# A GRU behind three residual layers on one core: the loads of the prologue in another order and on other queues, and one unit instead of two beside the z projection

## The chip, the core and the metric

The kernel runs on one core of one Trainium2 chip. A core has a TensorE (PE in the profile; PEld is its weight load), a VectorE (DVE), a ScalarE (ACT), a GpSimd (POOL) and a SyncE (SP), each of which works through its own instructions in the order in which the program lists them, and 16 DMA engines that are shared by all queues. The metric is the device time of one execution in microseconds; lower is better.

## The reference

The input x is 8 sequences of 512 tokens with 256 features. Four residual layers follow each other; three of them work on each token alone (given the conditioning vector of its sequence), the last is a recurrence over time.

```python
x = x + L0(x, cond)   # shared expert silu(x w1) * (x w3) w2, plus 8 experts gelu(x rw1) rw2,
                      # of which a router picks 2 for each token; all divided by 3
x = x + L1(x, cond)   # a Haar transform whose coefficients are all scaled by one gate(cond): x * (1 + gate)
x = x + L2(x, cond)   # x + gelu(x (down + low rank of cond)) (up + low rank of cond)
def step(H, xs):      # L3, for each of the 512 tokens
    xz, xr, xh = xs
    Z = sigmoid(xz + H @ Whz.T + bhz)
    R = sigmoid(xr + H @ Whr.T + bhr)
    H_tilda = tanh(xh + R * H @ Whh.T + bhh)
    H_new = Z * H + (1 - Z) * H_tilda
    return H_new, H_new @ Whq.T + bhq
x = x + L3(x)
```

## The kernel before

**Tiling.** Features lie on the partitions (two halves of 128), all 8 sequences are worked on together. Time is cut into 16 windows of 32 tokens (`WS`), so one window is 256 columns. L0 to L2 of one window are 72 *units* of TensorE work (`UNITS`): a unit is one call of `quads` (line 443 in its helper), four matmuls that fill the four column groups of the array, 8 matmul records with 256 columns in the trace. Layer 3 needs the windows in order, four tokens at a time.

**Two schedules.** The program is written out flat at build time. In the *prologue* (before line 1110) every instruction is a `Job` with its engine, its dependencies and the time that it is thought to take. `jobs.run(until)` plays a clock forward: each engine takes the first job of its list whose inputs are due by that clock, and the order so found is the order in the program. A load is thought to take `mb / RATE` us on its queue and to land `LAG` = 2.5 us later. The chip keeps this order, whatever the real times are: an engine whose next instruction waits does not look at the one behind it.

The prologue ends, in the plan, when window 0's last L0 matmul, the low-rank weights of L2 (`got_low_in`), the weights `wx` and `wh` and all 16 small loads `got_small` are done. Then the recurrence's own tiles are set up (lines 1110 to 1128 on DVE), window 0 is finished, three further PE jobs (`AHEAD`) are let through, the first two groups of four tokens are projected, and step 0 begins.

In the *loop*, each of the 512 steps lists its own chain, and fills the holes with jobs of later windows:

- matmuls of gate R (16 records, `grh<-wh,s_h`), sigmoid (line 1300), two transposes (1314), product with h (1331); matmuls of gate Z (16 records, `gz<-wh,s_h`) beside it;
- *first hole of PE*: one unit if `behind(s)`, and in every second step (`ahead` even) the part of the projection that feeds R and the candidate (8 records with 128 columns, `grh<-wx,xt`);
- matmuls of the candidate (16 records, `grh<-wh,s_rh`), tanh, transposes, and the scan (1390) that gives the new h;
- *second hole of PE*: in the other steps (`ahead` odd) z's part of the projection (8 records with 64 columns, `gz<-wx,xt`), and then two units if `behind(s)`, else one.

`behind(s)` is true while window 1 is unfinished, or while more units are left than a straight line that reaches zero near step 462 allows.

**Loads before.** All loads of the prologue are issued by SP (line 316), one after the other: `cond`, `rout`, `rbias` (small); x of windows 0 to 3 in two halves of 512 KB (`load_x`, rows of 512 B); `vec`, `b2` (small); `sw13` (two of 512 KB); `wsq_a` (1280 KB); `sw2`; `rw1`; `rw2`; eight pieces of `w2` (1024 KB each, line 316, into five buffers, so the sixth waits for a buffer that the first `generate` at line 1042 frees); `wx`, `wh`; 16 small loads (`h0`, `brows`, the recurrence's start and its biases); x of the other 12 windows.

**The route.** The router's logits of windows 0 to 3 (line 793) need all four windows of x; some 25 small DVE operations (lines 838 to 863) make the combination weights `s`, PE turns them (870), POOL writes them to DRAM (884) and fetches them back, broadcast (`bc`, 479). Every product of a routed expert on POOL (587) needs `bc`, and every unit `acc<-g,rw_sb` on PE needs such a product.

Of the kernel before, what the change touches and what calls it, by code (L numbers as in the profile page):

```python
# [9 lines left out]
F32 = mybir.dt.float32  # L10
# [6 lines left out]
P = 128  # L17
B, T, C = 8, 512, 256
KC = C // P
E = 8  # L20
HS = 512
HC = HS // P
R = 8
BR = B * R
WS = 32
# [7 lines left out]
FQ = C // NQ  # L33
# [18 lines left out]
EARLY = 4  # L52
# [4 lines left out]
LAST = 462  # L57
# [2 lines left out]
PE_ALONE, PE_WOVEN = 0.43, 0.65  # L60
LEAD = 20
AHEAD = 3
RATE = 0.35
LAG = 2.5


# [133 lines left out]
def cond_resid_kernel(  # L200
# [29 lines left out]
    nc = tc.nc  # L230
# [21 lines left out]
    const = ctx.enter_context(tc.tile_pool(name="const", bufs=1))  # L252
# [56 lines left out]

    jobs = Jobs()  # L310

    def load(out, in_, mb, lazies=(), deps=()):

        return jobs.add(
            "SP",
            lambda: nc.sync.dma_start(  # L316
                out=out.get() if isinstance(out, Lazy) else out, in_=in_
            ),
            deps,
            lazies,  # L320
            max(0.45, mb / RATE),
            lag=LAG,
        )

    def rows_of(m):
        return m.rearrange("(k p) o -> p k o", p=P)
# [3 lines left out]
    b2 = set1.tile([P, C], F32, name="b2")  # L330
# [3 lines left out]
    cond = const.tile([P, KC, B], F32, name="cond")  # L334
    rout = const.tile([P, 2, KC, E], F32, name="rout")
    vec = const.tile([P, 6, KC], F32, name="vec")
    rbias = const.tile([P, E], F32, name="rbias")
    got_cond = load(cond, condT, 0)
    got_rout = load(rout, router, 0)
    got_rbias = load(rbias, router_bias.broadcast_to([P, E]), 0)  # L340


    xw, xg, got_x = [], [], []
    xs, outs_ = [
        a.rearrange("(k p) (b t) -> p k b t", p=P, t=T) for a in (xT, outT)
    ]

    def load_x(n, mb):
        t0 = len(xw) * WS
        t = const.tile([P, KC, B, n * WS], F32, name=f"x{len(xg)}")  # L350
        xg.append((t0, t))
        for k in range(KC):
            got = load(t[:, k], xs[:, k, :, t0 : t0 + n * WS], mb)
        xw.extend(t[:, :, :, ts(i, WS)] for i in range(n))
        got_x.extend([got] * n)

    load_x(EARLY, 1.2)
    got_vec = load(vec, vecs, 0)
    got_b2 = load(b2[: 4 * R], bias2.rearrange("q (r d) -> (q r) d", d=C), 0)
    sw13_sb = const.tile([P, 2, KC, HS], F32, name="sw13_sb")  # L360
    got_sw13 = [load(sw13_sb[:, g], rows_of(sw13[g]), 0.5) for g in range(2)]
    wsq_a = const.tile([P, KC, 5, C], F32, name="wsq_a")
    got_sq_a = load(wsq_a.rearrange("p k n o -> p k (n o)"), rows_of(sq_a), 1.28)
    sw2_sb = const.tile([P, HC, C], F32, name="sw2_sb")
    got_sw2 = load(sw2_sb, rows_of(sw2), 0.5)
    rw1_sb = const.tile([P, KC, E, P], F32, name="rw1_sb")
    got_rw1 = load(rw1_sb.rearrange("p k e h -> p k (e h)"), rows_of(rw1), 1.0)
    rw2_sb = const.tile([P, E, C], F32, name="rw2_sb")
    got_rw2 = load(rw2_sb.rearrange("p e d -> p (e d)"), rw2, 1.0)

# [21 lines left out]
    h0 = const.tile([P, KC, B], F32, name="h0")  # L392
    brows = [const.tile([P, 3, FQ], F32, name=f"brow{n}") for n in range(2)]
    got_small = []
    for j in range(NQ):
        for i in range(KC):
            at_f = 64 * (j % 2) + 32 * i
            got_small.append(
                load(h0[ts(j, 32), i, :], condT[at_f : at_f + 32, j // 2, :], 0)
            )  # L400

        for n in range(2):
            row = bias_rows[:, 3 * n * C : 3 * (n + 1) * C].rearrange(
                "o (g f) -> o g f", g=3
            )[:, :, ts(j, FQ)]
            got_small.append(load(brows[n][ts(j, 32)], row.broadcast_to([32, 3, FQ]), 0))
    load_x(NW - EARLY, 1.8)


# [318 lines left out]
    def pe(fn, deps, lazies=(), takes=0.3):  # L728
        return jobs.add("PE", fn, deps, lazies, takes)

    def dve(fn, deps, lazies=(), takes=0.25):
        return jobs.add("DVE", fn, deps, lazies, takes)

    def act(fn, deps, lazies=(), takes=0.3):
        return jobs.add("ACT", fn, deps, lazies, takes)

    def flat(z):
        t = z.get()
        return t if len(t.shape) == 2 else t.rearrange("p a b -> p (a b)")
# [3 lines left out]
    j = dve(  # L743
        lambda: tt(
            prod,
            rout[:, 1].rearrange("p k (o e) -> p k o e", o=1).broadcast_to([P, KC, B, E]),
            cond.rearrange("p k (b o) -> p k b o", o=1).broadcast_to([P, KC, B, E]),
            ALU.mult,
        ),
        [got_cond, got_rout],  # L750
    )
# [12 lines left out]
    j = pe(time_bias, [j], [tb_ps])  # L764
# [141 lines left out]
    def mean_over_features(src, dep):  # L906
        ps = Lazy(r_c)

        def products():
            for k in range(KC):  # L910
                nc.tensor.matmul(
                    ps.get()[:, :B], inv_c, src[:, k, :], start=(k == 0), stop=(k == KC - 1)
                )

        return ps, pe(products, [dep], [ps])

    mu, j = mean_over_features(cond, got_cond)
    diff = set1.tile([P, KC, B], F32, name="diff")

    def center():  # L920
# [3 lines left out]
    j = dve(center, [j], [mu], 0.4)  # L924
    dsq = set1.tile([P, KC, B], F32, name="dsq")
    j = dve(lambda: tt(dsq, diff, diff, ALU.mult), [j])
    var_ps, j = mean_over_features(dsq, j)
    var = set1.tile([P, B], F32, name="var")
    j = dve(
        lambda: nc.vector.tensor_scalar(var, var_ps.get()[:, :B], EPS_LN, None, ALU.add),  # L930
        [j],
        [var_ps],
    )

    sd0 = set1.tile([P, B], F32, name="sd0")
    j = act(lambda: nc.scalar.activation(sd0, var, AF.Sqrt), [j], (), 1.6)
# [24 lines left out]
    def dense_cond(w, src, bias, name, dep):  # L961

        ps = Lazy(r_c)
        pre = set1.tile([P, KC, B], F32, name=f"{name}_pre")

        def out(m):
            return ps.get()[:, m * B : (m + 1) * B]

        def products():
            for m in range(KC):  # L970
                for k in range(KC):
                    nc.tensor.matmul(
                        out(m),
                        wsq_a[:, k, w, ts(m, P)],
                        src[:, k, :],
                        start=(k == 0),
                        stop=(k == KC - 1),
                    )

        def add_bias():  # L980
            for m in range(KC):
                nc.vector.tensor_scalar(
                    pre[:, m, :], out(m), vec[:, bias, m : m + 1], None, ALU.add
                )

        j = pe(products, [dep, got_sq_a], [ps], 0.6)
        return pre, dve(add_bias, [j, got_vec], [ps], 0.4)
# [6 lines left out]
    hid_pre, j = dense_cond(A_L2W1, lnc, V_BIAS1, "hid", got_lnc)  # L994
    hid_e, j = gated(hid_pre, AF.Erf, RSQRT2, "hid_e", j)
# [10 lines left out]
    g1_pre, j = dense_cond(A_L1W1, cond, V_B1, "g1", got_cond)  # L1006
    g1, j = gated(g1_pre, AF.Sigmoid, 1.0, "g1", j)
    j = dve(lambda: tt(g1, g1, g1_pre, ALU.mult), [j])
    gate_pre, j = dense_cond(A_L1W2, g1, V_B2, "gate", j)
    gate, j = gated(gate_pre, AF.Sigmoid, 1.0, "gate", j)  # L1010
# [8 lines left out]
    for n, of in enumerate(LOW):  # L1019
# [14 lines left out]
        j = pe(biased_rows, [got_b2], [gp], 0.45)  # L1034
        for k in range(KC):
            got = [pieces[q, k] for q in of]

            def generate(k=k, of=of, gp=gp):
# [12 lines left out]
            j = pe(  # L1051
                generate,
                [j, got_hid, *(g[1] for g in got)],
                [gp, *(g[0] for g in got)],
                1.75,
            )
        j = got_low_out[n] = dve(
            lambda n=n, gp=gp: nc.vector.tensor_copy(low_out[:, n], flat(gp)[:, :C]),
            [j],
            [gp],  # L1060
            0.45,
        )
# [8 lines left out]
        j = pe(turn, [j], [lt], 0.6)  # L1071
# [33 lines left out]
    with (  # L1105
# [14 lines left out]
        for u in range(GS):  # L1120
            s = gw.tile([P, KC, GS, B, 2], F32, name=f"s_h{u}")
            nc.vector.memset(s, 0.0)
            s_h.append(s)
            s = gw.tile([P, KC, GS, B], F32, name=f"s_rh{u}")
            nc.vector.memset(s, 0.0)
            s_rh.append(s)
            s = gw.tile([P, KC, B, 2], F32, name=f"d0_{u}")
# [133 lines left out]
        readers = {}  # L1261
        all_left = jobs.left("PE")

        def behind(s):
            return (
                any(j.done is None for j in ends[1])
                or jobs.left("PE") > all_left * (LAST - s) / (LAST + LEAD)
            )

        def late(s):  # L1270
# [12 lines left out]
        for c in range(NTC):  # L1283
            hist = hists[c]
            gates = upcoming
            for t in range(TC):
                s = c * TC + t
                n, u = t // GS, t % GS
                v = (u + 1) % GS
                rh, z = gates  # L1290
                now = base + s * STEP
# [28 lines left out]
                h = s_h[u][:, :, u, :, 1]  # L1320
# [3 lines left out]
                r, act_r = gate(rh[:, n, 0], AF.Sigmoid, "r", KC)  # L1324
# [27 lines left out]
                ahead = s + 5  # L1352
# [23 lines left out]
                cand, act_c = gate(rh[:, n, 1], AF.Tanh, "c", KC)  # L1376
                if part is not None:
                    part()
                jobs.fill("PE", now + 1.44, 2 if behind(s) else 1)
                if bias_parts and t >= 7:  # L1380
                    biased.append(bias_parts.pop(0)())
                    if not bias_parts:
# [27 lines left out]
                if c == NTC - 1 and t in (TC // 2 - 1, TC - TAIL - 1):  # L1410
                    a = 0 if t < TC // 2 else TC // 2
# [71 lines left out]
```

## Time and profile before

| what | us |
|---|---|
| median of 3 runs (1344.78, 1344.92, 1350.88) | 1344.92 |
| the profiled execution, its own time | 1344.15 |
| its span, first to last instruction | 1342.3 |
| first matmul of step 0 starts at | 71.90 |
| first matmul of step 511 starts at | 1334.07 |

Busy time of the span: PE 1176.8 us (88%), DVE 913.2 (68%), ACT 504.5 (38%), POOL 137.3 (10%). A share near 90% does not by itself say that PE sets the time: in the loop, PE can be busy with units that would fit elsewhere just as well. What sets the time is read stage by stage, from what ends last. The stages add up: 71.90 us of prologue, 1262.17 us for 511 steps (2.470 each), 8.23 us for the last step and the last stores, 1.85 us outside the span.

Granted PE clock and DMA, by stretch (the columns are the stretch, its length, busy us and count for each engine, then the granted clock, the mean share of the DMA engines and GB/s):

```profile
4.00:8.00 4.00, 2.86 (x20) 1.86 (x12) 1.09 (x7) 0.00 (x0) 0.00 (x0) 1.00 1.07 282
8.00:12.00 4.00, 3.43 (x145) 2.55 (x149) 2.73 (x14) 1.75 (x3) 0.00 (x0) 0.60 1.06 387
12.00:22.40 10.40, 7.87 (x121) 4.51 (x113) 6.00 (x32) 1.36 (x4) 0.00 (x0) 0.99 1.03 405
22.40:29.40 7.00, 6.50 (x60) 3.38 (x52) 2.16 (x9) 0.49 (x2) 1.82 (x3) 0.51 1.01 419
29.40:72.00 42.60, 39.93 (x728) 23.30 (x724) 12.06 (x43) 6.15 (x17) 8.11 (x12) 1.00 0.79 270
```

PE works at about half its clock from 22.4 to 29.4 us, and the DMA engines are full from 4 to about 30 us.

### The profile page before, as it was taken

The page shows a single profiled execution, that of the slowest core. Times are in us where ns is not written, and L with a number is a line of the kernel's source. Part 1 is how long each engine was busy: PE and PEld are TensorE (multiplying, and loading weights), DVE is VectorE, ACT ScalarE, POOL GpSimd, SP SyncE. Part 2 cuts the span into 40 slices and gives each one's busy share as a digit, 9 for nine tenths or more (in the row PEclk, how much of TensorE's full clock was granted, in tenths as well). Part 3 has the DMA queues.
Part 4 walks back from the last instruction along what each step waited for, and adds up shares of the span by engine and source line. Part 5 has one row for each costly group of instructions (what it writes and reads, how often), then busy time and mean ns, then how long its engine had stood idle before and what let it go on. Part 6 is the DMA issues. An engine that isn't in the chain of part 4 may idle for free.

```text
span 1342.3 us, 89396 instructions
## 1 busy us (share of the span) xinstructions
PE 1176.8 (88%) x39468; PEld 706.5 (53%) x39468; DVE 913.2 (68%) x6253; ACT 504.5 (38%) x3402; POOL 137.3 (10%) x203
## 2 busy tenths in 40 slices
PE   8999998989898989988898888889888888888885
PEld 4555555555555555554454545545555454545554
DVE  4266777776776767676676767667676766767675
ACT  1133334333343434334333433433343343433332
POOL 0211110101011110101011010101101010110000
PEclk8999999999999999999999999999999999999997
DMA  9731001100101010100101001010100100000111
GB/s 348 234 107 36 5 5 37 52 5 5 36 18 38 5 36 4 28 28 5 35 5 36 4 8 32 4 35 5 36 4 8 32 5 4 4 4 4 35 36 18
DMA packets 47093, 46.49 MB, mean 35 GB/s; under 512 B 24064, under 2 KB 44000, under 8 KB 45296
## 3 DMA queue, kind: packets, MB, share of 16 engines
q1 hardware_dynamic: 45344, 38.59, 9.3%
q8 instruction: 308, 5.05, 1.5%
q0 software_dynamic: 320, 2.13, 0.4%
q14 instruction: 81, 0.66, 0.2%
q10 hardware_dynamic: 1040, 0.07, 0.0%
HBM read 36.45 MB, written 4.33 MB: 30 GB/s over the span
## 4 chain that ended last, share of the span: by engine, by line
PE 68%; DVE 17%; ACT 8%; issue 5%; DMA 1%; SPq 1%; DVEq 0%; ACTq 0%
PE grh L1134 33%; PE hp L443 14%; PE acc L443 7%; DVE rT L1314 6%; PE gz L1134 5%; DVE d L1314 5%; PE low L443 5%; ACT r L1300 4%; PE misc L443 3%; ACT c L1300 3%; DVE s_rh L1331 2%; DVE s_h L1390 2%; SPq L316 1%; DMA wh<-in_sq_b_dram 1%; DMA x<-in_xT_dram 0%
## 5 line engine op out<-in xcount | busy, mean ns | idle before, releaser
L1300 ACT ACTIVATE r<-grh 128x32 f32<-128x32 f32 x1024 | 146.2, 195 | 443.2 <-PE grh L1134 443.2
L1314 DVE STREAM_TRANSPOSE rT<-r 128x32 f32<-128x32 f32 x1024 | 155.9, 190 | 227.6 <-ACT r L1300 224.3
L1134 PE MATMUL grh<-wh,s_h 128*32 128x64 f32 x8192 | 223.3, 226 | 78.6 <-DVE s_h L1390 76.3
L1134 PEld LDWEIGHTS grh<-wh,s_h 128*32 128x32 f32 x8192 | 143.5, 110 | 268.7 <-DVE s_h L1390 265.8
L1134 PE MATMUL grh<-wh,s_rh 128*32 128x64 f32 x8192 | 223.1, 226 | 57.6 <-DVE s_rh L1331 33.3
L1300 ACT ACTIVATE c<-grh 128x32 f32<-128x32 f32 x1024 | 146.2, 195 | 315.2 <-PE grh L1134 313.0
L1134 PEld LDWEIGHTS grh<-wh,s_rh 128*32 128x32 f32 x8192 | 141.1, 108 | 208.0 <-DVE s_rh L1331 202.1
L1314 DVE STREAM_TRANSPOSE d<-c 128x32 f32<-128x32 f32 x1024 | 156.6, 192 | 123.4 <-ACT c L1300 117.0
L1134 PE MATMUL gz<-wh,s_h 128*32 128x64 f32 x8192 | 211.3, 220 | 2.9 <-issue 2.9
L1134 PEld LDWEIGHTS gz<-wh,s_h 128*32 128x32 f32 x8192 | 154.8, 111 | 3.6 <-issue 3.6
L443 PE MATMUL hp<-x,sw_sb 128*32 128x256 f32 x2016 | 149.7, 385 | 3.6 <-issue 2.0
L443 PE MATMUL hp<-x,rw_sb 128*32 128x256 f32 x2016 | 151.0, 380 | 1.8 <-ACT sig L571 0.6
L587 POOL TENSOR_TENSOR g<-gl,bc 128x256 f32<-128x256 f32 x128 | 93.7, 733 | 546.7 <-DVE s_h L1390 379.5
L443 PE MATMUL acc<-g,rw_sb 128*32 128x256 f32 x2048 | 148.9, 379 | 0.0
L1390 DVE TENSOR_TENSOR_SCAN s_h<-d,d 128x16 f32<-128x16 f32 x1024 | 145.2, 184 | 0.0
L1331 DVE TENSOR_TENSOR s_rh<-rT,s_h 128x8 f32<-128x8 f32 x1024 | 133.5, 168 | 0.0
L1314 DVE STREAM_TRANSPOSE zT<-z 128x64 f32<-128x64 f32 x512 | 121.7, 238 | 2.9 <-ACT z L1300 2.9
L1300 ACT ACTIVATE z<-gz 128x64 f32<-128x64 f32 x512 | 121.0, 236 | 3.5 <-PE gz L1134 3.3
L1134 PE MATMUL grh<-wx,xt 128*32 128x128 f32 x2048 | 107.1, 274 | 3.1 <-ACT r L1300 3.1
L1404 ACT COPY hist<-s_h 128x16 f32<-128x16 f32 x512 | 106.1, 207 | 0.5 <-DVE s_h L1390 0.5
L1343 DVE TENSOR_TENSOR d<-zT,s_h 128x16 f32<-128x16 f32 x512 | 90.5, 177 | 17.6
L1344 DVE TENSOR_SCALAR d<-zT 128x16 f32<-128x16 f32 x512 | 86.6, 169 | 0.0
(150 smaller groups left out, 1185.5 us busy)
## 6 DMA issues: line engine op xcount, KB each, us to landing
bc<-comb_d SPq DMA_DIRECT2D x56, 256.0 KB, 4.4
w<-in_w_dram SPq DMA_DIRECT2D x8, 1024.0 KB, 17.2
out_dram<-x SPq DMA_DIRECT2D x14, 256.0 KB, 3.3
x<-in_xT_dram SPq DMA_DIRECT2D x2, 1536.0 KB, 9.7
rw_sb<-in_rw_dram SPq DMA_DIRECT2D x2, 1024.0 KB, 13.3
bc<-comb_d POOLq DMA_DIRECT2D x2, 1024.0 KB, 10.7
sw_sb<-in_sw_dram SPq DMA_DIRECT2D x3, 512.0 KB, 5.6
wsq_a<-in_sq_a_dram SPq DMA_DIRECT2D x1, 1280.0 KB, 9.5
```

The lines of the kernel that those rows point to most:

```text
L316: lambda: nc.sync.dma_start(out=out.get() if isinstance(out, Lazy) else out, in_=in_),
L443: nc.tensor.matmul(out[ts(j, 32)], lhs[:, ts(j, 32)], rhs, start=start, stop=False, skip_group_check=True,)
L587: lambda gl=gl, g=g, e=e: nc.gpsimd.tensor_tensor(g.get().rearrange("p (h t) -> p h t", t=P), gl.get().rearrange("p (h t) -> p h t", t=P), ...
L1134: nc.tensor.matmul(out[ts(j, 32)], lhs, rhs[:, ..., ts(j, FQ)], start=start, stop=False, skip_group_check=True,)
L1300: nc.scalar.activation(x, y, func)
L1314: ins = nc.vector.transpose(dst.rearrange("p i u b -> p i (u b)"), src.rearrange("p (i r) -> p i r", r=32),)
L1331: prod = tt(s_rh[u][:, k, u, :], rT[:, k, u, :], h[:, k], ALU.mult)
L1343: tt(d1[:, :, u, :, 1], zT[:, :, u, :], h, ALU.mult)
L1344: nc.vector.tensor_scalar(d0[:, :, :, 1], zT[:, :, u, :], -1.0, 1.0, ALU.mult, ALU.add)
L1390: new = nc.vector.tensor_tensor_scan(s_h[v][:, k, v].rearrange("p b w -> p (b w)"), d0[:, k].rearrange("p b w -> p (b w)"), d1[:, k, u].re ...
L1404: nc.scalar.copy(hist[:, :, t, :], s_h[v][:, :, v, :, 1])
```

## The change

Loads: the small ones of the start (`cond`, `rout`, `rbias`, `vec`, `b2`) go to ACT's queue, the 16 small ones of the end (`h0`, `brows`) to POOL's. On SP, window 0's x comes alone and first (two halves, rows of 128 B), then `sw13`, then x of windows 1 to 3 (rows of 384 B), then `rw1`, `sw2`, `wsq_a`, `rw2` (before: `wsq_a`, `sw2`, `rw1`, `rw2`). `RATE`, the planner's bandwidth, goes from 0.35 to 0.40. Loop: in the second hole, a step with z's part takes two units only if it is behind by more than 8 units (or window 1 is unfinished), else one.

```diff
-RATE = 0.35
+RATE = 0.40
...
-    def load(out, in_, mb, lazies=(), deps=()):
+    def load(out, in_, mb, lazies=(), eng="SP"):
+        issue = {"SP": nc.sync, "ACT": nc.scalar, "POOL": nc.gpsimd}[eng].dma_start
         return jobs.add(
-            "SP",
-            lambda: nc.sync.dma_start(
-                out=out.get() if isinstance(out, Lazy) else out, in_=in_
-            ),
-            deps,
+            eng,
+            lambda: issue(out=out.get() if isinstance(out, Lazy) else out, in_=in_),
+            (),
             lazies,
-            max(0.45, mb / RATE),
+            max(1.0 if eng == "POOL" else 0.45, mb / RATE),
             lag=LAG,
         )
...
-    got_cond = load(cond, condT, 0)
-    got_rout = load(rout, router, 0)
-    got_rbias = load(rbias, router_bias.broadcast_to([P, E]), 0)
+    got_cond = load(cond, condT, 0, eng="ACT")
+    got_rout = load(rout, router, 0, eng="ACT")
+    got_rbias = load(rbias, router_bias.broadcast_to([P, E]), 0, eng="ACT")
...
-    load_x(EARLY, 1.2)
-    got_vec = load(vec, vecs, 0)
-    got_b2 = load(b2[: 4 * R], bias2.rearrange("q (r d) -> (q r) d", d=C), 0)
+    x0 = const.tile([P, KC, B, EARLY * WS], F32, name="x0")
+    xg.append((0, x0))
+    xw.extend(x0[:, :, :, ts(i, WS)] for i in range(EARLY))
+    load_x(0, 0.25, (0, 1))
     sw13_sb = const.tile([P, 2, KC, HS], F32, name="sw13_sb")
     got_sw13 = [load(sw13_sb[:, g], rows_of(sw13[g]), 0.5) for g in range(2)]
+    load_x(0, 0.4, (1, EARLY))
+    got_vec = load(vec, vecs, 0, eng="ACT")
+    got_b2 = load(b2[: 4 * R], bias2.rearrange("q (r d) -> (q r) d", d=C), 0, eng="ACT")
+    rw1_sb = const.tile([P, KC, E, P], F32, name="rw1_sb")
+    got_rw1 = load(rw1_sb.rearrange("p k e h -> p k (e h)"), rows_of(rw1), 1.0)
+    sw2_sb = const.tile([P, HC, C], F32, name="sw2_sb")
+    got_sw2 = load(sw2_sb, rows_of(sw2), 0.5)
     wsq_a = const.tile([P, KC, 5, C], F32, name="wsq_a")
     got_sq_a = load(wsq_a.rearrange("p k n o -> p k (n o)"), rows_of(sq_a), 1.28)
-    sw2_sb = const.tile([P, HC, C], F32, name="sw2_sb")
-    got_sw2 = load(sw2_sb, rows_of(sw2), 0.5)
-    rw1_sb = const.tile([P, KC, E, P], F32, name="rw1_sb")
-    got_rw1 = load(rw1_sb.rearrange("p k e h -> p k (e h)"), rows_of(rw1), 1.0)
...
-                load(h0[ts(j, 32), i, :], condT[at_f : at_f + 32, j // 2, :], 0)
+                load(h0[ts(j, 32), i, :], condT[at_f : at_f + 32, j // 2, :], 0, eng="POOL")
...
-            got_small.append(load(brows[n][ts(j, 32)], row.broadcast_to([32, 3, FQ]), 0))
+            got_small.append(
+                load(brows[n][ts(j, 32)], row.broadcast_to([32, 3, FQ]), 0, eng="POOL")
+            )
...
-        def behind(s):
+        def behind(s, by=0):
             return (
                 any(j.done is None for j in ends[1])
-                or jobs.left("PE") > all_left * (LAST - s) / (LAST + LEAD)
+                or jobs.left("PE") > all_left * (LAST - s) / (LAST + LEAD) + by
             )
...
-                jobs.fill("PE", now + 1.44, 2 if behind(s) else 1)
+                two = behind(s, 8) or ahead % 2 == 0 and behind(s)
+                jobs.fill("PE", now + 1.44, 2 if two else 1)
```

## The prediction

> **What bounds the kernel now.** I cut the profiled execution at step 0 and step 511 (the starts of the first `grh<-wh,s_h` matmul of each, 71.90 and 1334.07 us) and ask of each stage what ends last.
>
> *The loop* comes first, since it holds 94% of the span. The chain of waits of the page gives most of it to PE:
>
> ```profile
> PE 68%; DVE 17%; ACT 8%; issue 5%; DMA 1%; SPq 1%; DVEq 0%; ACTq 0%
> ```
>
> That is a trap, and the timeline of PE alone, taken in a quiet stretch, shows it (columns: start, us, what, records; in brackets the idle time before and who ended it):
>
> ```profile
> 641.17 0.43 PE L1134 MATMUL grh<-wh,s_h 128*32 128x64 f32 x16 [0.36 <-DVE s_h L1390]
> ...
> 642.37 0.43 PE L1134 MATMUL grh<-wh,s_rh 128*32 128x64 f32 x16
> 642.62 0.29 PE L1134 MATMUL gz<-wx,xt 128*32 128x64 f32 x8
> 642.73 1.05 PE L443 MATMUL acc<-g,rw_sb 128*32 128x256 f32 x16
> 643.59 0.43 PE L1134 MATMUL grh<-wh,s_h 128*32 128x64 f32 x16
> ...
> 646.01 0.43 PE L1134 MATMUL grh<-wh,s_h 128*32 128x64 f32 x16 [0.36 <-DVE s_h L1390]
> ...
> 648.42 0.43 PE L1134 MATMUL grh<-wh,s_h 128*32 128x64 f32 x16 [0.24 <-DVE s_h L1390]
> ```
>
> Steps start at 641.17, 643.59, 646.01, 648.42: 2.42 us each, though the first has z's part and two units in its second hole, the third z's part and one. Over all steps the median is 2.418 and three quarters lie under 2.45. The recurrence's own chain sets the period; PE fills it. In the first of these steps the hole is exactly full: 0.25 + 0.11 + 2 x 0.43 = 1.22 us from the candidate's matmuls to the next step's, with no idle bracket. So 511 steps at 2.417 would be 1235.1 us; the trace has 1262.2. The 27.1 us between them are stalls: 23 steps longer than the median by over 0.3 us hold 20.8 of it. The wait table of PE in the loop names them:
>
> ```profile
> PE misc L793 <- issue: 5.4, 5, 1.8
> PE grh L1134 <- issue: 4.3, 7, 1.1
> PE gz L1134 <- issue: 4.3, 5, 1.3
> ```
>
> PE waits for nothing that the profile shows; only L793 (the routers) has a fixed place.
>
> *The prologue* is 71.9 us. From 8.91 us, when x's second half lands, PE has no idle of over 1.3 us; the largest that a load causes is at its end:
>
> ```profile
> 64.33 0.36 DVE L1110 TENSOR_TENSOR brow<-brow,brow 128x192 f32<-128x192 f32 x1 [1.10 <-DMA brow<-in_bias_rows_dram]
> ...
> 66.39 1.07 PE L443 MATMUL low<-u,low_out 128*32 128x256 f32 x16 [1.22 <-DVE u L645]
> ```
>
> DVE waits for the last of the 16 small loads, then sets up the recurrence's tiles, and only then makes `u`, for which PE has waited 1.22 us. The prologue is thus PE's own work (at half clock for about 10 us) behind a late start.
>
> **The change, part by part.**
>
> *Window 0's x alone and first.* SP's first x issue moves from 2.13 to 0.74 us, since three small issues (0.40, 0.42, 0.43) leave the queue. From the trace's packets, a row of 512 B takes 31.1 ns on one of 16 DMA engines: a half of x, 1024 rows, takes 1.99 us, and the halves landed at 7.03 and 8.87. So the flow began near 8.87 - 2 x 1.99 = 4.9, some 2.8 after the issue. Now it begins near 0.74 + 2.8 = 3.5. Rows of 128 B take 15.3 ns: 2048 of them 2.0 us, to 5.5. Each half of `sw13` follows in 1.33 (its landings before: 10.39, 11.72): 6.8 and 8.1. Here the Trainium skill speaks against the change: DMA: Bandwidth & Descriptors, Specifications, gives 512 B as the smallest transfer at line rate, with read-modify-write below. If a row of 128 B cost as much as one of 512 B, window 0 would take 4.0 us, `sw13` would land at 8.9 and 10.2, and PE would start no earlier than now. The trace has 15.3 against 31.1 ns: a quarter of the bytes for half the time. I take the row. PE begins its units at 6.8 instead of the routers at 8.91: **2.0 us earlier**. Some of this falls into the stretch from 8 to 12 us, where the granted clock is 0.60; I give back 0.5.
>
> *x of windows 1 to 3 behind `sw13`.* Rows of 384 B, between 20.0 ns (256 B) and 31.1: about 25.6, so 2048 rows take 3.3 us, to 11.4, against 8.87. The route starts 2.5 us later. Its cover: `s` is ready at 16.7 on DVE, but PE turns it at 20.84, 4.1 us later, because of what stands ahead in PE's queue. So POOL's write of `comb_d` stays near 22.6 and `bc`'s landing near 37.9; if the cover is gone, each us is paid once, since all eight expert products and 16 units queue behind `bc`. Cost 0; ends 0 and +5.
>
> *Weights reordered.* `wsq_a` goes behind `rw1` and `sw2`: 11.4 + 2.7 + 1.4 + 4.4 (the spacings of their landings before) = 20 us instead of 16.1. Its first user on PE stood at 19.27, and PE runs in order, so all units behind it wait: +0.5, between 0 and +1.5. The pieces of `w2` land where they did (first at 25.4), as the same bytes go ahead of them.
>
> *Five small loads on ACT.* A table load holds ACT from 0.75 to 2.03; if it stands first, `cond` lands 1.3 us later, at about 3.7. Its first matmul ran at 4.77, behind the zeroing matmuls, so nothing. Five issues of 0.43 end near 4.2; ACT's first own work is at 8.33. Cost 0.
>
> *Sixteen small loads on POOL.* At 0.54 to 0.71 us an issue (its three rows in the prologue) POOL is done by about 13 us, and is idle from 1.8 to 22.6: cost 0. On SP they are replaced by nothing; they stood from 49.98 to 62.8. The wait of 1.10 at 64.33 goes, and with it PE's 1.22. What is late next is DVE's set-up itself: the addition and 12 memsets take 64.33 to 65.7, and they move to the planned end of the prologue, which comes earlier, perhaps right ahead of the operations that end window 0's L0. +0.7, between 0 and +1.4. Net **-0.5**. `wh` (57.2) and `wx` have room.
>
> *RATE.* It moves no byte. It shortens the planned loads: 57.9 us on SP plus 2.5 before, about 42 after. Planned order is real order, so here lies most of the uncertainty.
>
> Prologue: -2.0 + 0.5 + 0.5 - 0.5 = **-1.5 us**, between -10 and +5. The clock adds to both ends: 22.4 to 29.4 ran at 0.51 and lost 3.4 us. TensorE: Matmul & The Clock Gate, Part 1, says that an idle window of about 3.4 us throttles and a busy one releases. By it the earlier, denser start would save up to those 3.4. But PE was busy for 7.87 of the 10.4 us ahead of that stretch, and was throttled all the same; I take no gain.
>
> *One unit instead of two beside z's part.* In a quiet step it saves nothing: both kinds last 2.42. Where a stall falls into the full hole, 0.43 us of room can take some of it up. 11 steps with z's part and two units have an excess in that hole; capped at 0.43 each it is 2.3 us. The units move to the other steps, whose second hole is 0.25 + 0.86 = 1.1 of 1.22: they fit. Enough units still pass: 2.2 a step are needed, 3 + 2 in two steps may go. **-2.0 us**. But every unit lands elsewhere, and the 14 us of "issue" waits are dealt anew: between -6 and +6.
>
> Sum -3.5: the profiled execution goes from 1344.15 to 1340.65, and as the median of the runs lies 0.8 above, I predict **1341.4**. A measurement of this kernel can tell 0.5%, 6.7 us, from no change.
>
> **Rivals.**
>
> *The plan shrinks the prologue.* Today it ends in the plan with the small loads, 60.4 us; without them with L0 and `wh`, near 45. If PE's order becomes denser, with nothing of window 1 in front of what step 0 needs (12 units, 5.2 us, stand there now) and part of the 3.9 us of idle between 11 and 40 us filled, 5 + 4 go on top of what I count: step 0 near 62, and 1344.9 - 10 = 1335. For it: the loop takes units free of charge. Against: 11 of the 12 run while window 0 waits for ACT, DVE or POOL. 0.28.
>
> *The route comes late* (the slower side). If x of windows 1 to 3 at 11.4 and `wsq_a` at 20 push the turn of `s` past 20.84, `comb_d` is written later than 22.6, and `bc` lands later than 37.9. PE now reaches `acc<-g,rw_sb` at 40.24, so 2 us earlier than that it is just in time; beyond, each us stalls PE in order. With 5 us of delay the prologue loses 3, and with stalls dealt badly (+4) the time is 1352. It decides once `comb_d`'s issue is later than about 25 us. 0.12.
>
> *Nothing starts earlier.* Short rows cost as the rule says, and the loop stays: 1344 to 1345. 0.15.
>
> **How the numbers follow.** The forecast itself has 0.45. From its spread 0.05 goes to faster by over 0.5%, to which the first rival adds 0.28: 0.33. Slower is the second rival, 0.12, and the rest of the forecast and the third rival is within 0.5%: 0.55. The range, 1331.5 to 1349, takes in the first rival with a lucky loop and half of the second.
>
> **What would show it.** Right: first `hp<-x,sw_sb` near 6.8; `comb_d`'s issue within 1 us of 22.6; no wait for `brow`; step 0 at 68 to 72; median step 2.42; sum of stalls 20 to 31 us. Wrong: step 0 at or under 65 (first rival) or over 73; a median step other than 2.42, which would mean that PE did set the period.

## The result, and the profile after

| | before | after |
|---|---|---|
| median of 14 runs each, us | 1349.81 (1342.62 to 1351.75) | 1342.1 (1338.05 to 1352.72) |
| ratio to before, 95% interval | | 0.9961 [0.9943, 0.9979] |
| same kernel, a second comparison | 1346.71 | 1342.51: 0.9973 [0.9954, 0.9991] |
| profiled execution: step 0 at | 71.90 | 71.81 |
| 511 steps | 1262.17 | 1256.01 |
| last step and stores | 8.27 | 8.45 |
| median step; sum of what lies above 2.417 | 2.418; 27.1 | 2.417; 20.9 |

The kernel is faster by 0.4% [0.2%, 0.6%], some 5 us; the second comparison gives 3.6. (The medians lie 7.7 us apart, since the runs of the kernel before scatter widely; the means are 1348.14 and 1342.79, and the ratio is close to theirs.) The gain is real, since the interval leaves 1 out, and below 0.5%, which the prediction took as what can be told in one measurement.

In these two profiles all of it is in the loop, and nothing in the prologue, though the prologue is what most of the change is about. The two profiles are no average, though: 1338.05 us is the fastest of the 14 runs after, and 1344.15 is faster than most runs before. The page's chain of waits reads as before:

```profile
PE 69%; DVE 16%; ACT 8%; issue 4%; DMA 1%; ACTq 0%; DVEq 0%
```

PE's timeline of the kernel after, in a quiet stretch (start, us, what, records; idle before and its releaser in brackets):

```profile
662.34 0.43 PE L1144 MATMUL grh<-wh,s_h 128*32 128x64 f32 x16
...
663.78 0.29 PE L1144 MATMUL gz<-wx,xt 128*32 128x64 f32 x8
...
664.75 0.43 PE L1144 MATMUL grh<-wh,s_h 128*32 128x64 f32 x16 [0.68 <-DVE s_h L1401]
...
667.17 0.43 PE L1144 MATMUL grh<-wh,s_h 128*32 128x64 f32 x16 [0.79 <-DVE s_h L1401]
...
668.62 0.29 PE L1144 MATMUL gz<-wx,xt 128*32 128x64 f32 x8
668.73 0.60 PE L453 MATMUL misc<-mid,low_in 128*32 128x256 f32 x4
669.59 0.43 PE L1144 MATMUL grh<-wh,s_h 128*32 128x64 f32 x16 [0.26 <-DVE s_h L1401]
```

The steps start 2.41, 2.42 and 2.42 us apart, with 0.68, 0.79 or 0.26 us of idle in front of them: the period doesn't depend on how full the hole is.

In the prologue the same work runs in another order, to the same end. PE's timeline after:

```profile
8.04 1.08 PE L453 MATMUL misc<-b,pick 128*32 128x256 f32 x8 [0.81 <-DMA b<-in_bias_dram]
8.87 1.96 PE L453 MATMUL hp<-x,sw_sb 128*32 128x256 f32 x16
10.58 0.64 PE L803 MATMUL grh<-rout,x 128*32 128x8 f32 x32
15.58 1.23 PE L803 MATMUL grh<-rout,x 128*32 128x8 f32 x96
...
27.62 0.30 PE L880 MATMUL grh<-ident,s 128*64 128x128 f32 x1
...
46.13 1.71 PE L1052 MATMUL misc<-w,hid 128*32 128x256 f32 x26 [1.39 <-DMA w<-in_w_dram]
```

The first unit on x starts at 8.87, where the routers started at 8.91 and the first unit at 11.37 before. Of the routers' 128 records, 96 now run at 15.58, so the turn of `s` (L880) is at 27.62 instead of 20.87. POOL's timeline of both kernels, before and after, shows the route that follows from it:

```profile
22.59 0.71 POOL L884 DMA_DIRECT2D comb_d<-cT  x1 [20.78 <-DVE cT L878]
38.08 2.80 POOL L587 TENSOR_TENSOR g<-gl,bc 128x256 f32<-128x256 f32 x4 [8.81 <-DMA bc<-comb_d]
```

```profile
28.53 0.56 POOL L894 DMA_DIRECT2D comb_d<-cT  x1 [15.71 <-DVE cT L888]
33.74 1.12 POOL L489 DMA_DIRECT2D bc<-comb_d  x2 [4.65 <-DMA comb_d<-cT]
39.37 0.73 POOL L597 TENSOR_TENSOR g<-gl,bc 128x256 f32<-128x256 f32 x1 [4.51 <-DMA bc<-comb_d]
```

`comb_d` leaves 5.9 us later, but POOL's first product only 1.3 us later, as the first fetch of `bc` takes 5.5 us from issue to landing instead of 9.8: two pieces of `w2` have still to land when it is issued, where it was three. At the end of the prologue the small loads' wait is gone: DVE's timeline after has no bracket at the bias addition.

```profile
54.77 0.35 DVE L1120 TENSOR_TENSOR brow<-brow,brow 128x192 f32<-128x192 f32 x1
```

### The profile page after: what moved, and what is told of

It is laid out like the page before. It is cut to its first block, busy times and chain, and to the rows that moved or that the text cites. A ratio compares the mean times of both kernels' runs of the same rounds, so it can differ in the third digit from the quotient of the medians.

```text
span 1336.3 us, 89415 instructions
## 1 busy us (share of the span) xinstructions
PE 1184.2 (89%) x39468; PEld 706.8 (53%) x39468; DVE 912.9 (68%) x6253; ACT 506.9 (38%) x3403; POOL 145.6 (11%) x219
## 4 chain that ended last, share of the span: by engine, by line
PE 69%; DVE 16%; ACT 8%; issue 4%; DMA 1%; ACTq 0%; DVEq 0%
PE grh L1144 34%; PE hp L453 15%; PE acc L453 7%; DVE rT L1324 6%; DVE d L1324 5%; PE gz L1144 5%; ACT r L1310 4%; PE low L453 4%; ACT c L1310 3%; PE misc L453 3%; DVE s_rh L1341 2%; DVE s_h L1401 2%; DMA w<-in_w_dram 1%; PE misc L1052 0%; DMA b<-in_bias_dram 0%
## 6 DMA issues: line engine op xcount, KB each, us to landing
wsq_a<-in_sq_a_dram SPq DMA_DIRECT2D x1, 1280.0 KB, 11.6
```

## The experiments

Each kernel is compared with runs of the kernel before on the same chip; kernels of one comparison shared them. The table has the ratio with its 95% interval, and from one profile each: step 0, the excess of all 511 steps over 2.417 us, the number of three-unit steps among 96 to 460 that follow another one ("pairs"), and the number of windows at half clock in the loop.

| kernel | ratio | step 0 | excess | pairs | half-clock windows |
|---|---|---|---|---|---|
| before | | 71.90 | 27.1 | 68 | 1 |
| before_again | one run, 1344.44 us | 69.90 | 29.3 | 68 | 5 |
| loads_only | 1.0003 [0.9987, 1.0019] | 73.60 | 29.7 | 69 | 6 |
| small_only | 0.9986 [0.9967, 1.0005] | 70.52 | 28.1 | 69 | 4 |
| loop_only | 0.9979 [0.9965, 0.9994] | 70.54 | 26.2 | 29 | 6 |
| one_beside_rh | 0.9978 [0.9966, 0.9991] | 71.33 | 29.9 | 29 | 6 |
| two_a_step | 0.9950 [0.9934, 0.9966] | 70.48 | 26.7 | 40 | 5 |
| bursts | 1.0011 [0.9994, 1.0028] | 73.64 | 33.9 | 128 | 9 |
| after | 0.9961 [0.9943, 0.9979] | 71.81 | 20.9 | 23 | 3 |
| after_again | 0.9973 [0.9954, 0.9991] | 70.48 | 24.6 | 23 | 5 |
| x_ahead_of_sw13 | 0.9976 [0.9959, 0.9993] | 72.16 | 27.7 | 23 | 7 |
| small_and_loop | 0.9954 [0.9939, 0.9969] | 71.45 | 28.0 | 23 | 6 |
| routers_apart | 0.9953 [0.9934, 0.9971] | 74.62 | 18.7 | 34 | 2 |
| small_two_routers | 0.9914 [0.9890, 0.9938] | 71.76 | 20.7 | 55 | 4 |

Two profiles of one program differ by 2 us in the prologue and by up to 4 in the loop, so a single profile can't rank these kernels; the ratios do that, and the profiles say which waits came and went. The intervals of loads_only, small_only and bursts take in 1: none of these three is shown to differ from the kernel before.

### Which half of the change does it

The two halves, each put alone into the kernel before, and the kernel before once more.

```diff
loop_only, loads_only is the rest of the change:
-        def behind(s):
+        def behind(s, by=0):
...
-                or jobs.left("PE") > all_left * (LAST - s) / (LAST + LEAD)
+                or jobs.left("PE") > all_left * (LAST - s) / (LAST + LEAD) + by
...
-                jobs.fill("PE", now + 1.44, 2 if behind(s) else 1)
+                two = behind(s, 8) or ahead % 2 == 0 and behind(s)
+                jobs.fill("PE", now + 1.44, 2 if two else 1)
```

> The kernel before with the loop's edit alone (one unit beside z's part). Theory A (room beside z's part swallows PE's instruction stalls): step 0 at 71.9 us as before, excess of the steps 96 to 460 over 2.417 us falls from 12.8 to about 6, time 0.995 to 0.997 of before. Theory B (any change of the order deals the stalls anew, and the loads' part did it): excess anywhere between 8 and 18, ratio 0.998 to 1.003. Theory C (the prologue's loads brought the gain): no change.

> The changed kernel with two units beside z's part again, so only the loads and RATE are changed. Theory A: step 0 at 71.8 us, excess of the steps 96 to 460 near 12.8, time 0.999 to 1.001 of before. Theory B: excess between 8 and 18. Theory C: ratio near 0.996.

> The kernel before once more, for its profile: are the stalls in the same steps? Theory A and D: the long stalls (over 0.3 us) fall in the same steps as in the first profile, within a few, and the excess is 27 us give or take 1.5. If they are chance of the single execution: other steps, and an excess that differs by several us.

The loop's edit alone brings 2.8 us (0.9979 of 1346.29), the loads alone nothing (1.0003). The kernel before, profiled once more, has 15 of its first profile's 23 long steps (over 0.3 us above the median) again, so most stalls have a fixed place and some don't. It shows step 0 at 69.90 instead of 71.90. One difference is the row of the stretch from 22.4 to 29.4 us, which stood at a clock of 0.51 above. It reads here, and below it in the kernel after (stretch, length, busy us and count of PE, PEld, DVE, ACT, POOL, granted clock, DMA share, GB/s)

```profile
22.40:29.40 7.00, 6.33 (x88) 3.71 (x80) 2.87 (x11) 0.74 (x4) 1.77 (x3) 1.00 1.03 426
22.40:29.40 7.00, 5.87 (x94) 2.84 (x86) 2.93 (x13) 3.13 (x5) 0.56 (x1) 1.00 1.01 413
```

Full clock and 88 records instead of 60. The half clock there belongs to the execution and not to the kernel: of the six profiles with the old prologue (before, before_again, loop_only, one_beside_rh, two_a_step, bursts) three have it and three don't. It also costs less than it seems. loop_only and two_a_step have no half clock in the old prologue and reach step 0 at 70.54 and 70.48; with 10.2 us of it the kernel before needs 71.90. The kernel after has none in either profile and needs 71.81 and 70.48. At equal clock, then, the new prologue is no faster than the old one.

### Room beside z's part, or evener filling

The mirror image: the full hole stays where z's part is, and the step without it gets one unit.

```diff
-                jobs.fill("PE", now + 1.44, 2 if behind(s) else 1)
+                two = behind(s, 8) or ahead % 2 == 1 and behind(s)
+                jobs.fill("PE", now + 1.44, 2 if two else 1)
```

> The kernel before with the edit turned round: one unit in the second hole of the steps that carry the R and candidate part, two beside z's part. Theory A (room is needed in the full hole): the hole beside z's part is full more often, excess of steps 96 to 460 is 12 or more, ratio 1.000 to 1.003. Theory D (fewer steps with three units, wherever the units are missing): excess falls as in the changed kernel, ratio near 0.996.

It gains as much (0.9978 against 0.9979), with 113 of its three-unit steps beside z's part, where loop_only has 17. So it isn't the 0.43 us of room beside z's part. What both share is a more even filling: pairs fall from 68 to 29. Two more kernels push that in both directions. The first takes a second unit at that place only when 8 units behind, whatever the step; the second takes none unless behind or late, so that the units come in bursts.

```diff
two_a_step:
+                two = behind(s, 8)
+                jobs.fill("PE", now + 1.44, 2 if two else 1)
bursts:
+                jobs.fill("PE", now + 1.44, 2 if behind(s) or late(s) else 0)
```

> The kernel before with one unit instead of two in the second hole of every step, unless it is over 8 units behind: mostly two units a step, seldom three. Theory D (fewer steps with three units, wherever they are missing, since a thinned step has room): gains more than the changed loop, ratio 0.994 to 0.997. Theory A (only the room beside z's part counts): as loop_only, 0.998. Theory B (dealt anew by chance): 0.998 to 1.002.

> The changed kernel once more, on the same chip as the next three. If the loads add nothing (loads_only was 1.0003) and the loop's edit is all (loop_only 0.9979): ratio 0.9965 to 0.999. If both parts add up to the first result: 0.996. Step 0 of the profile between 70 and 74 us.

> The kernel before with the opposite of an even filling: three units in a step that is behind, none in one that is not. The number of steps with three units rises by about a fifth. Theory D: slower, ratio 1.001 to 1.004. Theory B: 0.998 to 1.002, on either side. If the period were PE's own in full steps, it would be slower by more than 1%.

Even filling is the fastest of the four (0.9950), bursts the slowest (1.0011, and no faster than the kernel before). The profiles show two separate costs.

*At full clock.* I took the steps from 97 to 460 that no half-clock window touches. In the four profiles with the old filling (before, before_again, loads_only, small_only) their excess is 11.2, 9.9, 8.6 and 10.9 us; in the six with the change's filling or its mirror (loop_only, one_beside_rh, after, after_again, x_ahead_of_sw13, small_and_loop) 6.9, 8.3, 5.5, 7.4, 6.0 and 6.8. The two sets, formed after the runs, only just keep apart (8.6 and 8.3), and two profiles of the kernel after differ by 1.9; the means, 10.2 and 6.8, are 3.4 us apart, which is the size of the measured 2.8. So the edit's gain probably lies at full clock. Pairs don't explain it: over all profiles a three-unit step behind another one has an excess of 0.040 us, any other step 0.02, which makes 40 fewer pairs worth only 0.8 us; and bursts, with 128 pairs, has 8.4 us here, less than the old filling. Some 2 of the 3.4 us lie in steps in which, or right ahead of which, PE waits for instructions (see the routers' stalls below): these hold 5.4 us on average with the old filling and 3.4 with the new. The rest is open, and so is why the new order has fewer such waits.

*At half clock.* A stretch of before_again in the middle of the loop, PE's timeline:

```profile
665.07 0.43 PE L1134 MATMUL grh<-wh,s_h 128*32 128x64 f32 x16 [0.36 <-DVE s_h L1390]
...
667.49 0.55 PE L1134 MATMUL grh<-wh,s_h 128*32 128x64 f32 x16 [0.68 <-DVE s_h L1390]
668.23 0.67 PE L1134 MATMUL grh<-wx,xt 128*32 128x128 f32 x8
669.22 1.49 PE L443 MATMUL misc<-mid,low_in 128*32 128x256 f32 x6
670.25 0.43 PE L1134 MATMUL grh<-wh,s_h 128*32 128x64 f32 x4
...
673.40 0.43 PE L1134 MATMUL grh<-wh,s_h 128*32 128x64 f32 x16
```

The second and the third of these steps last 2.76 and 3.15 us instead of 2.42. The windows of the same kernel say what happened (columns as above):

```profile
660.88:664.29 3.41, 3.30 (x118) 2.00 (x112) 2.33 (x18) 1.16 (x10) 0.00 (x0) 1.00 0.02 5
664.29:667.70 3.41, 1.83 (x77) 1.08 (x73) 2.21 (x17) 2.01 (x11) 0.00 (x0) 1.00 0.02 5
667.70:671.11 3.41, 3.41 (x76) 2.27 (x68) 2.29 (x14) 1.16 (x7) 0.00 (x0) 0.50 0.02 5
671.11:674.53 3.42, 3.29 (x126) 2.01 (x118) 2.50 (x17) 1.30 (x10) 0.00 (x0) 1.00 0.01 2
```

The step at 665.07 holds no unit, PE is busy for 1.83 of 3.41 us, and the next 3.41 us run at a clock of 0.50. All 14 profiles agree: each of the 69 half-clock windows of the loops (of 3.4 or 6.8 us) follows 3.4 us in which PE was busy for 0.56 of the time or less, and within one execution all of them begin on one grid of 3.413 us, to within 6 ns. TensorE: Matmul & The Clock Gate, Part 1, of the Trainium skill describes such a free-running window of 4096 cycles; what the loop adds is that the stretch ahead needn't be idle, half busy is enough. So a kernel with light steps is exposed by as much as it has such stretches, and each execution meets them by the phase of its grid: one profile of the kernel before has one window, the other five. Of the steps that would have lain wholly inside such a window at 2.417 us, the 12 with three units are 1.60 us longer on average, the nine with one unit 0.48. In bursts, 17.3 of the 33.9 us of excess lie in the steps that its nine windows touch. If a stretch of 3.413 us is laid at every place of the loop but its last steps, less than 0.553 of it (near the largest share seen ahead of a half-clock window) is busy in 2.3% of the places for the kernel before, which is 8.2 stretches a run, whatever the phase. It is 9.9 for bursts, 8.2 for loop_only, 4.5 for one_beside_rh and 4.3 for two_a_step: loop_only doesn't lessen the exposure, two_a_step halves it.

An estimate from these numbers: 69 of 112 such stretches were throttled, and the steps touched have 1.51 us of excess for each window, so an exposed stretch costs 0.93 us. two_a_step saves 3.9 of them, 3.6 us, and has 7.7 instead of 10.2 us at full clock: 6.1 together, and 6.7 were measured. For loop_only it gives a gain of 3.3 where 2.8 were measured, for bursts a gain of 0.2 where 1.5 were lost, for one_beside_rh 5.3 against 3.0, where it is too much. It is a rule of thumb, no more.

### The routers' stalls

PE's waits in the loop, kernel after (what waits, for what, us in total, times, longest): the routers wait for no other engine and no load of the kernel.

```profile
PE misc L803 <- issue: 5.9, 5, 2.0
PE gz L1144 <- issue: 1.9, 3, 1.0
```

They come in rows of many small records. In the kernel after the planner puts several such jobs of 8 columns behind each other, 128 records in some 5 us; the edit counts each as done 2.2 us later, so that the next one, which depends on it, is planned apart from it.

```diff
-            d = pe(
+            d = jobs.add(
+                "PE",
...
+                lag=0.0 if via_pool else 2.2,
```

> The changed kernel with the routers' products of a window (32 matmul records with 8 columns) at least 2.2 planned us apart, so that no two windows' products stand in one step. In the profile after, the steps 27 to 29, 59 to 61 and 91 to 92 exceed the median by 9.4 us in sum. If the cost comes from several such jobs in one hole: sum falls to 2 to 5 us, and the time by 4 to 7 us, ratio to before 0.991 to 0.995. If each job pays its own stall: sum stays at 7 to 10, ratio as after_again.

The wait at that line falls to 0.7 us, but `gz` takes more (PE's waits of routers_apart):

```profile
PE misc L803 <- issue: 0.7, 2, 0.4
...
PE gz L1146 <- issue: 4.8, 5, 2.4
```

The excess of the steps in which windows' routers run (26 to 33, 58 to 63, 90 to 95) is 5.3 us, against 9.4 and 7.7 in the two profiles of the kernel after. The ratio, 0.9953 against 0.9973, lies in the right direction with overlapping intervals: probable, not shown.

What starves PE is in the traces after all. The page of either kernel has a DMA queue of its own for instructions:

```profile
q8 instruction: 308, 5.05, 1.5%
```

Its 308 packets of 16 KB are one for each 128 of PE's 39,468 matmul records, or for each 256 of its instructions, as every matmul has a weight load of its own. In the loops of the 14 profiles, PE has 156 waits of over 0.3 us that are put down to "issue". Every one of them, the routers' and the others', stands at the same place of a block of 128 matmuls (number 87 or 88, counted from the program's first), and ends 1.19 to 1.61 us after a packet of this queue has arrived; a moment taken at random in the loop of the kernel before lies so behind a packet in 10% of cases. PE's timeline of the longest one in the kernel after:

```profile
224.66 0.28 PE L803 MATMUL misc<-rout,x 128*32 128x8 f32 x13
226.90 0.33 PE L803 MATMUL misc<-rout,x 128*32 128x8 f32 x18 [1.97 <-issue]
```

The packet for it ran from 224.52 to 225.40. So these stalls are PE waiting for its next block of instructions. That is also why moving the routers apart moved part of the stall to `gz`: the wait stands at the block's edge, whatever operation is there. What makes a packet late enough to be waited for wasn't tested.

### Why the loads bring nothing

The late route was the suspect, so x of windows 1 to 3 was put ahead of `sw13` again.

```diff
     load_x(0, 0.25, (0, 1))
+    load_x(0, 0.4, (1, EARLY))
     sw13_sb = const.tile([P, 2, KC, HS], F32, name="sw13_sb")
     got_sw13 = [load(sw13_sb[:, g], rows_of(sw13[g]), 0.5) for g in range(2)]
-    load_x(0, 0.4, (1, EARLY))
```

> The changed kernel with x of windows 1 to 3 right behind window 0's x, ahead of sw13. If the loads gain nothing because the route starts late (comb_d's issue at 28.5 us in the changed kernel, 22.4 to 23.0 in the kernels with the old loads): comb_d is issued at 21 to 25 us, PE no longer waits for pieces of w2 at 44 to 51 us, step 0 without a half clock falls from 70.5 to 71.8 to 67 to 70, ratio to before 0.994 to 0.997. If PE's own work sets the prologue and the route does not matter: comb_d early, but step 0 at 70 to 72, ratio as the changed kernel, 0.996 to 0.998.

The route comes back, as POOL's timeline of it shows, and the time does not (0.9976, no better than the kernel after; step 0 at 72.16, without half clock):

```profile
22.36 0.56 POOL L894 DMA_DIRECT2D comb_d<-cT  x1 [10.82 <-DVE cT L888]
```

PE's timeline of the same kernel has a wait for a piece of `w2` instead, 1.81 us, where the kernel after has 1.39 at 46.13:

```profile
43.95 1.71 PE L1052 MATMUL misc<-w,hid 128*32 128x256 f32 x26 [1.81 <-DMA w<-in_w_dram]
```

But the early route hadn't made PE any busier before that. Two stretches of the kernel after, then the same of this one (columns as above):

```profile
8.00:22.00 14.00, 12.73 (x260) 7.11 (x264) 5.11 (x20) 1.41 (x4) 3.21 (x6) 1.00 1.08 365
22.00:40.00 18.00, 16.64 (x265) 9.82 (x257) 7.80 (x40) 6.00 (x13) 2.32 (x4) 1.00 0.96 398
```

```profile
8.00:22.00 14.00, 12.42 (x245) 6.78 (x241) 6.41 (x30) 2.57 (x5) 2.73 (x6) 1.00 1.04 374
22.00:40.00 18.00, 16.92 (x262) 9.84 (x258) 7.34 (x34) 3.96 (x11) 3.62 (x6) 1.00 1.01 418
```

PE is idle for 2.6 us of these 32 in the one and for 2.7 in the other. The route was late, but other units filled the time. The other suspect is the small loads. They were moved alone, on top of the kernel before (small_only) and on top of loop_only; large loads and `RATE` stay as before.

```diff
-    got_cond = load(cond, condT, 0)
+    got_cond = load(cond, condT, 0, eng="ACT")
...
-    got_b2 = load(b2[: 4 * R], bias2.rearrange("q (r d) -> (q r) d", d=C), 0)
+    got_b2 = load(b2[: 4 * R], bias2.rearrange("q (r d) -> (q r) d", d=C), 0, eng="ACT")
...
+                load(h0[ts(j, 32), i, :], condT[at_f : at_f + 32, j // 2, :], 0, eng="POOL")
```

> The kernel before with the loop's edit and with the 21 small loads on ACT's and POOL's queues; the large loads in the old order, RATE 0.35. If the late small loads cost what the prediction says (net 0.5 us, at most 1.2): no wait for brow, PE's idle of 1.2 to 1.5 us ahead of low<-u gone or shortened, step 0 without a half clock at 69 to 70 (loop_only: 70.5), ratio 0.9970 to 0.998. If the planned end, now earlier, makes PE's order better: step 0 at 66 to 69.

> The kernel before with only the 21 small loads on ACT's and POOL's queues; the loop, RATE and the large loads as before. small_and_loop was 0.9954, loop_only 0.9979, loads_only 1.0003. If the small loads gain and the new order of the large ones gives it back: ratio 0.996 to 0.999, no wait for brow. If the small loads give nothing, since PE's wait near 8 us (2.9 us in small_and_loop) takes back what the end gains: 0.999 to 1.001, and the difference of small_and_loop from loop_only was the order in the loop, or chance.

Their wait at the end is gone in both, but the start pays: the first unit on x begins at 14.18 and 13.43 us, where it was 11.37. PE's timeline of small_and_loop:

```profile
10.16 1.08 PE L442 MATMUL misc<-b,pick 128*32 128x256 f32 x8 [2.93 <-DMA b<-in_bias_dram]
```

PE waits 2.93 us for `b2`, which landed at 10.02 on ACT's queue instead of at 9.06 to 9.23 on SP's. x's second half lands at 9.83, and in small_only at 8.64, against 8.69 to 8.87 with the old queues, though it was issued 1.4 us earlier. The small loads' packets now stand between its own on the 16 DMA engines; how much of the lost start is theirs wasn't measured apart. The ratios, 0.9986 alone (the interval takes in 1) and 0.9954 against loop_only's 0.9979 from another comparison, make a small gain probable. Since small loads and loop together (0.9954) are no slower than the whole change (0.9961, 0.9973), nothing shows a gain from the new order of the large loads with `RATE`.

### What adds up

two_a_step, the small loads and the routers' lag in one kernel, large loads as before:

> Small loads on ACT and POOL, two units a step, the routers' products apart; large loads as before. If the parts add (two_a_step 0.995, routers_apart 0.9953 to after_again's 0.9973, small loads 0.0005): 0.992 to 0.994. If they swallow the same stalls: 0.9945 to 0.996.

0.9914 [0.9890, 0.9938], 11.6 us less than the kernel before and the best of all. Its interval lies below 1 and below both of the kernel after's.

## Why the prediction was right, step by step

The sign and the size came out: -3.5 us forecast, -5.3 measured and -3.6 in the second comparison. That the time itself did so to 0.7 us (1342.1, forecast 1341.4) is in part luck, since the forecast started from 1344.92, the median of three runs, and the kernel before measured 1349.81 in the comparison. The parts did not come out: -1.5 for the loads and -2.0 for the loop were forecast, and each alone measures 0 and -2.8. Whether both together give more than their sum the intervals leave open.

- **The chain sets the period**: shown. The median step is 2.417 to 2.419 us in all 14 profiles, with units spread evenly or in bursts.
- **The loop's -2.0**: size right (2.8 alone), mechanism wrong. "0.43 us of room" in the full hole was to take up stalls; one_beside_rh keeps those holes full and gains the same. What the runs put in its place: an evener filling, with the gain probably at full clock; in part it is fewer waits of PE for its next block of instructions, and the rest is open. These are the "issue" stalls of which the prediction said that only the routers' have a fixed place: all of them stand at the edge of a block.
- **The prologue's -1.5**: wrong, it is 0. The failing term is "PE begins its units at 6.8": they begin at 8.87. x of window 0 landed at 5.52 (forecast 5.5), and its rows of 128 B took 13.0 ns each, those of 384 B 25.0 (forecast 15.3 and 25.6; the 15.3 was a mean of 2181 records, 2048 of them stores much later in the run, while loads of that size took 12.4). A short row costs more for its bytes than a long one, but far less than a row of 512 B, so the weighing of row against rule held. What failed is that `sw13` followed at once, at 6.8 and 8.1: it landed at 8.09 and 9.68. A unit on `b2`, which landed at 7.91, stands ahead in PE's order and took until 8.87. The loads that were costed at nothing on ACT and POOL account for some 0.6 us of each DMA engine up to 8.09, which is part of the 1.3 by which `sw13` was late; the rest isn't resolved. Hidden issue on an idle engine isn't hidden transfer.
- **The route at no cost**: the cover of 4.1 us was wrongly taken as fixed. The turn of `s` moved from 20.87 to 27.62 because the planner set 96 router records behind other units, and `comb_d`'s issue at 28.53 is past the 25 us from which the second rival was to decide. Its price wasn't paid: `bc` landed at 39.23 and 41.71 instead of 37.94 and 40.41, 1.3 us later and not 5.9, since less stood ahead of it on the DMA engines by then.
- **wsq_a** landed at 21.48, forecast 20, `w2`'s first piece at 26.55, forecast 25.4: 1.5 and 1.2 us late, about as much as `sw13` (1.3 and 1.6).
- **The small loads' wait**: gone, as forecast, with PE's 1.22 us.
- **The half-clock give-back**: 22.4 to 29.4 was read as a property of the kernel (PE "was throttled all the same"). A second profile of the same program ran it at full clock. Nor did it cost the 3.4 us that the prediction names: old prologues without half clock reach step 0 only 1.4 us earlier. "PE was busy for 7.87 of the 10.4 us" also says less than it seems. The last 3.41 us ahead of the half clock in the kernel before, and the next 3.40:

```profile
19.09:22.50 3.41, 2.44 (x37) 1.67 (x33) 2.00 (x11) 0.22 (x1) 0.00 (x0) 1.00 1.00 414
22.50:25.90 3.40, 3.40 (x28) 2.31 (x24) 1.43 (x6) 0.00 (x0) 0.71 (x1) 0.50 0.99 414
```

The first stretch counts as busy for 2.44 us, but holds only 37 records.

- **The first rival** (step 0 near 62): no prologue came below 69.9.

## What to carry to other kernels

Where a chain of small dependent operations sets the period, fill its holes evenly: here two units in most steps beat the old mixture, and a stretch of 3.4 us left half empty was often followed by half clock, in which the dense steps overran. When PE idles with nothing to wait for, count its records between the stalls: a fixed distance (here 128 matmuls) points to the loading of instructions. A load on an idle queue costs no issue time, but its bytes still pass the same DMA engines: moving small loads off the first large ones' queue isn't enough if they still run beside them. And profile a program twice before a throttled stretch, or 2 us of one stage, is taken as its own.

## What the runs showed of the hardware that was not expected

- The clock's windows: a grid of 3.413 us per execution, half clock after a window with PE busy for 0.56 or less in the loop (69 of 69). It isn't sufficient: 43 such windows were followed by full clock. In the prologue the busy share is no such guide: the 3.41 us ahead of 22.50 in the kernel before show 2.44 us busy (0.71), with 37 records, and half clock followed; perhaps matmuls that wait for their data are drawn as busy.
- PE's instructions arrive in packets of 16 KB, one for 128 matmuls and their weight loads, and all 156 of its waits of over 0.3 us without another cause stand at the edge of such a block, up to 2.4 us each.
- ACT's DMA issues ran ahead of its first table load in the kernel after: `cond` was issued at 0.75 us, the table load stood at 3.42.
- An issue on POOL held it for 0.51 to 0.68 us in the kernel after, a small one on SP for 0.40 to 0.43 at the start of the kernel before.
